# Loading and splitting the first block of a three-pass fp32 matmul kernel in smaller pieces

## The chip, the core and the metric

The kernel runs on one core of one Trainium2 chip. The metric is the device time of one execution in microseconds (us); of several runs the median is given. Beside the runs there is one profiled execution, whose trace is read here.

## What is computed

`x` is 64 samples of 64 channels by 1024 values, so 4096 rows of 1024. Each sample has a condition, which picks one of 16 matrices of 64 x 64. The reference, cut to what matters:

```python
y = einsum('bct,bcd->bdt', x, W[condition])            # mixes the 64 channels of a sample
logits = einsum('bsd,ed->bse', y, gate_w)              # 8 experts, the best 2 are kept
weights = softmax(top_k(logits, 2))                    # w_full: 8 numbers a row, 6 of them zero
result = einsum('bsd,od->bso', y, base_w) + base_b     # 1024 x 1024
low = einsum('bsd,erd->ebsr', y, lora_A)               # 8 experts x rank 16
lora = einsum('ebsr,eor,bse->bso', low, lora_B, w_full)
out = x + result + 2.0 * lora
```

## The kernel before

The mixing of channels is applied after the large product, since it acts on the other side of x. For each tile of 128 rows (two samples; there are 32 tiles) the kernel first forms z = x times one wide matrix of 1160 columns: 136 for the low-rank part and the gate, then the 1024 of `base_w`. It is cut into three column blocks of 384, 388 and 388 (`CN`; `W` is 388), and its 1024 rows into four quarters of 2 x 128 (`KQ` = 4). A weight block "b21" is quarter 2, column block 1, held as 128 partitions x 2 slices x 388 columns; a slice is one set of 128 rows, index `f` in the code. Likewise an x block is 128 partitions x 2 slices x 128.

Every fp32 operand is split into a high part, a copy rounded to the matmul's fp32r type, and a low part, the difference. Each product is then three matmuls into the same PSUM bank: high x times high weights, high x times low weights, low x times high weights. In the profile `xr` is x as loaded, `xh` and `xl` its parts; `w_b` is a weight block as loaded, `wh_b` and `wl_b` its parts. Line 232 is the copy that makes a high part (ScalarE, or VectorE for the first x blocks), line 229 the subtraction that makes a low part (VectorE), line 409 the three matmuls of z.

The first four tiles are multiplied plainly; the other 28 go in pairs through a 2 x 4 by 4 x 3 block product with fewer multiplications, made of sums of the blocks (line 290 for x, line 340 for weights). After z, line 441 mixes the channels and adds the low-rank part, line 492 is a transpose for it, and line 451 or 232 brings the result into `xtok`, from which it is stored.

The order on each engine is not written by hand. Steps are registered with `add(engine, cost, fn, reads, writes, ...)` in class `Program`; `reads` and `writes` are keys of buffers, from which it derives what depends on what. `run` then simulates the engines with the costs given and always issues, on the engine that comes free first, the step that is due earliest. Only after that are semaphores set. A key stands for the unit on which steps wait for each other: before the change an x block has one key, ("xr", u), and a weight block one key for each of its two slices, ("w", slot, f).

At the start, tiles 0 and 1 run together: for each quarter, column blocks 1 and 2, tile 0 before tile 1. The loads of the first weight block, b11, are issued from ScalarE's queue, one for each slice (line 319); all others and the loads of x (line 274) are issued from SP's queue, first the two x blocks of quarter 1, then the two slices of b12, then from b21 on alternately a weight block (line 324) and an x block. Behind the last weight blocks but one stands the load of `lb` (lora_B, into an `xtok` buffer, line 589), then eight loads of x for tiles 2 and 3, and then the last weight block, b23. Each transfer from these two queues takes one of eight completion semaphores in turn, so a load also waits until the transfer eight before it has landed. While the first data come, `NWARM` = 39 small matmuls on zeros (line 223) keep TensorE at work.

Of the kernel before, what the change touches and what calls it, by code (L numbers as in the profile page):

```python
# [20 lines left out]
P = 128  # L21
# [10 lines left out]
W = 388  # L32
N0 = NG + T - 2 * W
CN = (N0, W, W)
OUTS = ((NG, N0, 0), (0, W, N0 - NG), (0, W, N0 - NG + W))
KQ = 4
NPAIR = NT // 2
NPLAIN = 2
# [3 lines left out]
PE, ACT, DVE, POOL, SP = "PE", "ACT", "DVE", "POOL", "SP"  # L42
# [4 lines left out]
ISSUE = 0.45  # L47
# [30 lines left out]
class Program:  # L78
# [7 lines left out]
    def add(self, engine, cost, fn, reads=(), writes=(), due=None, first=False, size=0.0, early=None, port=False,  # L86
            after=0.0):

        n = len(self.steps)
        engine, cost = (e if isinstance(e, (list, tuple)) else [e] for e in (engine, cost))
        deps = set()
        for b in list(reads) + list(writes):
            if b in self.writer:
                deps.add(self.writer[b])
        for b in writes:
            deps.update(self.readers.get(b, ()))
        for b in reads:
            self.readers.setdefault(b, []).append(n)  # L100
        for b in writes:
            self.writer[b], self.readers[b] = n, []
        deps.discard(n)
        self.steps.append(dict(eng=dict(zip(engine, cost)), fn=fn, deps=deps, first=first, size=size, port=port,
                               lag=FLIGHT + QUEUE + size * DMA if size else 0.0, after=after,
                               due=self.horizon if due is None else due,
                               early=SP in engine and not reads if early is None else early))
# [59 lines left out]
def cond_ffn_kernel(ctx, tc, xT, x, idx, cw, wall, bias, lb, out):  # L167
# [21 lines left out]
    nc = tc.nc  # L189
# [4 lines left out]
    def many(n, shape, dt, name):  # L194
# [6 lines left out]
    xr = sb.tile([P, NXR, 2 * P], F32, name="xr")  # L201
    xh, xl = sb.tile([P, NXA, 2 * P], F32R, name="xh"), sb.tile([P, NXA, 2 * P], F32R, name="xl")
# [8 lines left out]
    bank = {nm: ps.tile([P, 512], F32, name=f"ps_{nm}")  # L211
            for nm in ("z0", "z1", "z2", "z3", "a0", "a1", "o0", "o1")}
# [13 lines left out]
    add = pr.add  # L226

    def sub(e, o, a, b):
        eng[e].tensor_tensor(o, a, b.bitcast(F32), ALU.subtract)  # L229

    def copy(e, o, a):
        (nc.scalar.copy if e == ACT else nc.vector.tensor_copy)(o, a)  # L232
# [7 lines left out]
    def tt_cost(n):  # L240
        return 0.08 + 0.00104 * n
# [22 lines left out]
    def some(t, us):  # L264

        a, b = us[0], us[-1]
        if len(us) == 1 or a < b:
            return t[:, a:b + 1:max(1, b - a)]
        return t[:, a:a + 1].broadcast_to([P, 2, t.shape[2]])


    def load_x(i, k, u):

        add(SP, ISSUE, lambda e: nc.sync.dma_start(  # L274
            xr[:, u].rearrange("p (k n) -> p k n", k=2), xT[i][:, 2 * k:2 * k + 2]), writes=[("xr", u)],
            size=8.0 * P * P)

    def split_x(us, hi=ACT):

        n = len(us)  # L280
        js = xas.two() if n == 2 else [xas.one()]
        add(hi, 0.1 + (0.115 if hi == ACT else 0.09) * 2 * n, lambda e: copy(e, some(xh, js), some(xr, us)),
            [("xr", u) for u in us], [("xh", j) for j in js])
        add(DVE, tt_cost(2 * P * n), lambda e: sub(e, some(xl, js), some(xr, us), some(xh, js)),
            [("xr", u) for u in us] + [("xh", j) for j in js], [("xl", j) for j in js], port=True)
        return js

    def sum_x(os, xs, ys, f):

        add(DVE, tt_cost(2 * P * len(os)), lambda e: nc.vector.tensor_tensor(some(xr, os), some(xr, xs), some(xr, ys), f),  # L290
            [("xr", u) for u in set(xs + ys) - set(os)], [("xr", u) for u in os], port=True)


    class Block:


        def __init__(self, name, dt=F32):
            self.name, self.dt, self.slot, self.t = name, dt, slots.one(), None
            self.keys = [("w", self.slot, f) for f in range(2)]

        def ap(self):
            if self.t is None:
# [3 lines left out]
    raw, hi, lo = {}, {}, {}  # L306
# [4 lines left out]
    def load_w(m):  # L311

        k, n = int(m[1]) - 1, int(m[2]) - 1
        b = raw[m] = Block(f"w_{m}")
        if k == 0 and n < 2:

            for f in range(2):
                q, dma = (SP, nc.sync.dma_start) if n else (ACT, nc.scalar.dma_start)
                add(q, ISSUE, lambda e, f=f, dma=dma: dma(b.ap()[:, f:f + 1], wall[k][n][:, f:f + 1]),
                    writes=b.keys[f:f + 1], size=4.0 * P * W, early=False)  # L320
            if not n:
                add(ACT, 1.5, lambda e: nc.scalar.activation(warm, warm, AF.Exp))
            return
        add(SP, ISSUE, lambda e: nc.sync.dma_start(b.ap(), wall[k][n]), writes=b.keys, size=8.0 * P * W, early=False)  # L324

    def split_w(m, p, step=2):

        b, h, l = raw[m], Block(f"wh_{m}_{p}", F32R), Block(f"wl_{m}_{p}", F32R)
        hi[p], lo[p] = h, l
        for j in range(0, 2, step):  # L330
            a = slice(j, j + step)
            add(ACT, 0.2 + 0.00083 * W * step, lambda e, a=a: copy(e, h.ap()[:, a], b.ap()[:, a]), b.keys[a], h.keys[a])
            add(DVE, tt_cost(W * step), lambda e, a=a: sub(e, l.ap()[:, a], b.ap()[:, a], h.ap()[:, a]),
                b.keys[a] + h.keys[a], l.keys[a], port=True)
# [25 lines left out]
    SINGLE = dict(b32="p1", b42="p2", b41="p12", b33="p11", b31="p20")  # L360
# [36 lines left out]
    due = {}  # L397

    def mm_cost(n):
        return max(COL * n + SET, LEAST)  # L400

    def zstep(key, b, j, p, f, start, stop, cols=W):


        z, n = bank[b][:, :cols], slice(f * P, (f + 1) * P)

        def do(e):
            for q, (l, w) in enumerate(((xh, h), (xh, g), (xl, h))):
                nc.tensor.matmul(z, l[:, j, n], w.ap()[:, f, :cols], start=(start and q == 0), stop=(stop and q == 2),  # L409
                                 skip_group_check=True)  # L410
        h, g = hi[p], lo[p]
        add(PE, 3 * mm_cost(cols), do, [("xh", j), ("xl", j), h.keys[f], g.keys[f]], [b, "order"], due=due[key])

    def split_z(n, src, key):

        q = take("zq", NZ)
        h, l = zh[q][:, :n], zl[q][:, :n]
        add(ACT, 0.2 + 0.00085 * n, lambda e: copy(e, h, src()), [key], [("zh", q)])
        add(DVE, 0.09 + 0.00104 * n, lambda e: sub(e, l, src(), h), [key, ("zh", q)], [("zl", q)],
            port=isinstance(key, tuple))  # L420
        return q

    def outs(c):

        lo, hi, o = OUTS[c]
        return slice(lo, hi), slice(o, o + hi - lo)
# [98 lines left out]

    PLAIN = [(i, c, k) for k in range(KQ) for c in range(2) for i in range(2)]
    PLAIN += [(i, 2, k) for i in range(2) for k in LASTK]
    for q in range(1, NPLAIN):
        PLAIN += [(i, c, k) for c in range(3) for i in (2 * q, 2 * q + 1) for k in range(KQ)]
    t = 4.9  # L530
# [23 lines left out]
    xa0 = {}  # L554
# [8 lines left out]
    def load_split_x(i, k, **how):  # L563
        u = xrs.one()
        load_x(i, k, u)
        xa0[i, k], = split_x([u], **how)
        xrs.give(u)

    for k in range(KQ):
        for i in range(2):  # L570
            load_split_x(i, k, hi=DVE if k == 0 else ACT)
            load_split_w(f"b{k + 1}{i + 1}", step=1 if k == 0 else 2)

    chan = sb.tile([P, 1], F32, name="chan")
# [20 lines left out]
    zb, left = {}, {}  # L595
# [3 lines left out]
    def plain(i, c, k):  # L599
        if (i, k) not in xa0:  # L600
            us = xrs.two()
            for d in range(2):
                load_x(i, k + d, us[d])
            xa0[i, k], xa0[i, k + 1] = split_x(us)
            xrs.give(*us)
        if (i, c) not in zb:
            zb[i, c] = f"z{take('z', 4)}"
            if c == 0 and i > 1:
                load_cond(i)
        ks, m = LASTK if c == 2 and i < 2 else range(KQ), f"b{k + 1}{c + 1}"  # L610
        for f in range(2):
            zstep(("plain", i, c, k, f), zb[i, c], xa0[i, k], SINGLE.get(m, m), f, k == ks[0] and f == 0,
                  k == ks[-1] and f == 1, CN[c])
        left[i, k] -= 1
        if not left[i, k]:
            xas.give(xa0[i, k])
        if k == ks[-1]:
            post(i, c, split_z(CN[c], lambda: bank[zb[i, c]][:, :CN[c]], zb[i, c]))
            if c == 2:
                late_sum(i)  # L620
                store(i, range(3))
# [74 lines left out]
    z = {nm: bank[b][:, :W] for nm, b in BANKS.items()}  # L696
# [153 lines left out]
```

## Time and profile before

| | us |
|---|---|
| median of 3 runs | 460.23 |
| lowest and highest | 459.87, 460.57 |
| profiled execution, its whole time | 460.46 |
| span of its trace | 458.7 |
| TensorE busy | 452.3 (99%) |
| VectorE busy | 383.4 (84%) |
| ScalarE busy | 227.5 (50%) |
| first matmul of z starts | 5.04 |
| first matmul of tile 1 starts | 7.11 |

Times within the trace count from the start of the span. In the profile PE is TensorE, PEld its weight loads, DVE is VectorE, ACT is ScalarE, POOL is GpSimd and SP the sync engine; PEq, ACTq and SPq are their sequencers, and a DMA on such a line is its issue. An instruction's line gives its start, its duration, the engine, the line of the kernel, the operation, and what it writes and reads; in brackets stands how long the engine was idle before it, and who ended that. Durations of matmuls overlap, so their pace is read from their starts.

### The profile page before, as it was taken

To read this page: it belongs to the slowest core of one execution; us is meant where nothing else is said; L and a number is where in the kernel's file an instruction comes from. 1 tells how busy PE (TensorE), PEld (TensorE's weight loads), DVE (VectorE), ACT (ScalarE), POOL (GpSimd) and SP (SyncE) were. 2 spreads that over 40 slices of the span, in tenths; PEclk is the share of its full clock that TensorE was granted. 3 is DMA by queue.
4 is the path that set the end of the run, shared out by engine and by line. 5 is a ranking of instruction groups with operands and counts; after the bars stand their busy time and mean duration, and the time that the engine had idled before them with its cause. 6 is when DMAs were issued, how large, how long until landed. Compare 5 with 4: busy or idle time off the path is not lost.

```text
span 458.7 us, 7562 instructions
## 1 busy us (share of the span) xinstructions
PE 452.3 (99%) x2615; PEld 449.0 (98%) x2615; DVE 383.4 (84%) x940; ACT 227.5 (50%) x520; POOL 88.8 (19%) x107
## 2 busy tenths in 40 slices
PE   8999999999999999999999999999999999999995
PEld 8999999999999999999999999999999999999995
DVE  5999997878989788796997979789797988888674
ACT  5864656543636345373543646355354544546231
POOL 3010215121303021120303003030120403103000
PEclk9999999999999999999999999999999999999999
DMA  8942739976778462764846566573655746456142
GB/s 284 336 126 42 160 98 205 214 215 198 176 211 202 172 161 88 215 128 167 188 137 189 119 185 150 172 181 110 196 120 177 182 128 195 114 176 148 48 137 91
DMA packets 36085, 75.00 MB, mean 164 GB/s; under 512 B 4416, under 2 KB 22096, under 8 KB 36048
## 3 DMA queue, kind: packets, MB, share of 16 engines
q0 software_dynamic: 10560, 36.72, 33.7%
q1 hardware_dynamic: 25200, 37.41, 26.0%
q10 hardware_dynamic: 288, 0.40, 0.3%
q8 instruction: 20, 0.33, 0.3%
q14 instruction: 17, 0.14, 0.1%
HBM read 57.74 MB, written 16.78 MB: 162 GB/s over the span
## 4 chain that ended last, share of the span: by engine, by line
PE 93%; DMA 5%; DVE 1%; SPq 1%; ACT 0%; issue 0%; ACTq 0%
PE ps_z L409 71%; PE ps_o L441 15%; PE ps_a L441 6%; DMA xtok<-in_lb 2%; DMA w_b<-in_w 2%; DMA xr<-in_xT 1%; PE ps_a L492 1%; SPq L324 0%; SPq L274 0%; DVE xtok L451 0%; DVE wl_b_b L229 0%; ACT wh_b_b L232 0%; DVE st L727 0%; ACTq L232 0%
## 5 line engine op out<-in xcount | busy, mean ns | idle before, releaser
L229 DVE TENSOR_TENSOR xl<-xr,xh 128x512 fp32r<-128x512 f32 (+1 forms) x138 | 92.3, 672 | 20.6 <-ACT xh L232 20.3
L409 PE MATMUL ps_z<-wh_t_p,xh 128*128 128x388 f32 (+1 forms) x308 | 105.3, 342 | 0.1
L409 PE MATMUL ps_z<-wl_t_p,xh 128*128 128x388 f32 (+1 forms) x308 | 104.3, 339 | 0.0
L409 PE MATMUL ps_z<-wh_t_p,xl 128*128 128x388 f32 (+1 forms) x308 | 104.3, 339 | 0.0
L232 ACT CAST xh<-xr 128x512 fp32r<-128x512 f32 (+1 forms) x136 | 82.5, 610 | 37.4 <-PE ps_z L409 32.8
L727 DVE TENSOR_TENSOR st<-ps_z,st 128x388 f32<-128x388 f32 x126 | 70.3, 559 | 21.0 <-PE ps_z L409 19.9
L290 DVE TENSOR_TENSOR xr<-xr 128x256 f32<-128x256 f32 (+1 forms) x139 | 69.7, 528 | 3.1 <-DMA xr<-in_xT 2.7
L409 PE MATMUL ps_z<-wh_b_p,xh 128*128 128x388 f32 (+1 forms) x180 | 61.4, 341 | 0.0
L409 PE MATMUL ps_z<-wh_b_p,xl 128*128 128x388 f32 (+1 forms) x180 | 60.8, 338 | 0.0
L409 PE MATMUL ps_z<-wl_b_p,xh 128*128 128x388 f32 (+1 forms) x180 | 60.8, 338 | 0.0
L409 PEld LDWEIGHTS ps_z<-wh_t_p,xh 128*128 128x128 f32 x308 | 57.8, 188 | 1.2 <-DVE st L727 0.7
L409 PEld LDWEIGHTS ps_z<-wl_t_p,xh 128*128 128x128 f32 x308 | 57.9, 188 | 0.0
L409 PEld LDWEIGHTS ps_z<-wh_t_p,xl 128*128 128x128 f32 x308 | 57.8, 188 | 0.0
L458 POOL DMA_DIRECT2D out<-xtok x30 | 16.8, 560 | 193.5 <-DVE xtok L451 92.2
L232 ACT CAST zh<-st 128x388 fp32r<-128x388 f32 (+1 forms) x70 | 36.2, 517 | 24.2 <-DVE st L727 17.0
L376 POOL DMA_DIRECT2D xtok<-in_bias x28 | 27.4, 980 | 97.3 <-DMA xtok<-in_x 90.0
L389 POOL DMA_INDIRECT bdr<-in_cw,rows x32 | 36.1, 1129 | 28.0 <-DVE zl L229 16.6
L710 ACT ACTIVATE ps_z<-ps_z 128x388 f32<-128x388 f32 x42 | 20.1, 478 | 41.1 <-PE ps_z L409 39.0
L451 DVE TENSOR_TENSOR xtok<-ps_o,xtok 128x388 f32<-128x388 f32 x56 | 31.0, 559 | 11.0 <-PE ps_o L441 10.6
L229 DVE TENSOR_TENSOR zl<-st,zh 128x388 fp32r<-128x388 f32 (+1 forms) x70 | 38.9, 556 | 1.5 <-ACT zh L232 1.2
L409 PEld LDWEIGHTS ps_z<-wh_b_p,xh 128*128 128x128 f32 x180 | 33.8, 188 | 0.2
L409 PEld LDWEIGHTS ps_z<-wl_b_p,xh 128*128 128x128 f32 x180 | 33.8, 188 | 0.0
(130 smaller groups left out, 871.1 us busy)
## 6 DMA issues: line engine op xcount, KB each, us to landing
xr<-in_xT SPq DMA_DIRECT2D x128, 128.0 KB, 3.1
xtok<-in_bias POOLq DMA_DIRECT2D x32, 512.0 KB, 7.2
out<-xtok POOLq DMA_DIRECT2D x30, 512.0 KB, 3.1
xtok<-in_x SPq DMA_DIRECT2D x28, 512.0 KB, 3.7
w_b<-in_w SPq DMA_DIRECT2D x10, 388.0 KB, 5.8
xtok<-in_x POOLq DMA_DIRECT2D x4, 512.0 KB, 6.2
out<-xtok SPq DMA_DIRECT2D x4, 194.0 KB, 2.5
bdr<-in_cw,rows POOLq DMA_INDIRECT x32, 5.3
```

What stands on the lines that cost most here:

```text
L229: eng[e].tensor_tensor(o, a, b.bitcast(F32), ALU.subtract)
L232: (nc.scalar.copy if e == ACT else nc.vector.tensor_copy)(o, a)
L290: add(DVE, tt_cost(2 * P * len(os)), lambda e: nc.vector.tensor_tensor(some(xr, os), some(xr, xs), some(xr, ys), f), [("xr", u) for u in s ...
L376: add(POOL, 1.1, lambda e: nc.gpsimd.dma_start(xtok[j], bias.broadcast_to([P, T]), accum_op=ALU.add), writes=keys, size=TWICE * 4.0 * T * P)
L389: add(POOL, 1.04, lambda e: nc.gpsimd.indirect_dma_start(out=bdr[j], out_offset=None, in_=cw, in_offset=bass.IndirectOffsetOnAxis(ap=rows[ ...
L409: nc.tensor.matmul(z, l[:, j, n], w.ap()[:, f, :cols], start=(start and q == 0), stop=(stop and q == 2), skip_group_check=True)
L441: nc.tensor.matmul(d, l, r, start=(start and m == 0), stop=(stop and m == len(mms) - 1), skip_group_check=True)
L451: add(DVE, 0.09 + 0.00104 * (s.stop - s.start), lambda e: nc.vector.tensor_tensor(xtok[j][:, o], bank[b][:, s], xtok[j][:, o], ALU.add), [ ...
L458: add(POOL, 1.0, lambda e: nc.gpsimd.dma_start(out[i * P:(i + 1) * P, o], xtok[j][:, o]), src, size=4.0 * P * (o.stop - o.start))
L492: add(PE, 0.107, lambda e: nc.tensor.matmul(tp, low[i % 2][:, :ER], ident, is_transpose=True, start=False, stop=False, skip_group_check=True),
L710: add(ACT, 0.2 + 0.00085 * W, lambda e: nc.scalar.mul(z[b], z[x], scale), [BANKS[x]], [BANKS[b]])
L727: add(DVE, 0.09 + 0.00104 * W, lambda e: nc.vector.tensor_tensor(unit(u), a(), b(), f), reads, [ukey(u)])
```

## The change

Slice 0 of the first weight block, b11, is treated as two halves of 194 columns; slice 1 stays whole. So b11 is loaded in three transfers instead of two, cast in three copies and subtracted in three subtractions. The first x block, tile 0 of quarter 1, is loaded as two slices of 128 in two transfers, cast in two copies on VectorE and subtracted in two. For tile 0 the three matmuls of b11's slice 0, 384 wide, become six of 194 (the four columns beyond 384 are padding). For that the keys are made finer: an x block has a key for each slice, a weight slice one for each half, and `add` accepts lists of keys. Everything else waits on all of the finer keys and does the same work as before. `NWARM` and the costs of all other steps are unchanged.

In the order that the planner makes of it, ScalarE issues the loads of b11 as first half of slice 0, slice 1, second half of slice 0, and casts and subtractions of b11 follow in the same sequence. TensorE's matmuls go first half, second half, slice 1. SP's queue has one transfer more at its head and ScalarE's one more at its own. One copy on ScalarE (`bdh`, the first tile's channel matrix) stands one weight block earlier than before. The rest of the program has the same order on every engine.

```diff
+HALVES = (slice(0, 194), slice(194, W))
...
+        reads, writes = ([k for q in ks for k in (q if isinstance(q, list) else [q])] for ks in (reads, writes))
...
     def load_x(i, k, u):
-        add(SP, ISSUE, lambda e: nc.sync.dma_start(
-            xr[:, u].rearrange("p (k n) -> p k n", k=2), xT[i][:, 2 * k:2 * k + 2]), writes=[("xr", u)],
-            size=8.0 * P * P)
+        for a, n in ((0, 1), (1, 1)) if (i, k) == (0, 0) else ((0, 2),):
+            add(SP, ISSUE, lambda e, a=a, n=n: nc.sync.dma_start(
+                xr[:, u, a * P:(a + n) * P].rearrange("p (k n) -> p k n", k=n),
+                xT[i][:, 2 * k + a:2 * k + a + n]), writes=xkeys("xr", [u])[a:a + n], size=4.0 * n * P * P)
...
+        if parts:
+            for f in range(2):
+                c, k, x, y, z = slice(f * P, (f + 1) * P), 0.1 + 0.09, ("xr", us[0], f), ("xh", js[0], f), ("xl", js[0], f)
+                add(hi, k, lambda e, c=c: copy(e, xh[:, js[0], c], xr[:, us[0], c]), [x], [y])
+                add(DVE, tt_cost(P), lambda e, c=c: sub(e, xl[:, js[0], c], xr[:, us[0], c], xh[:, js[0], c]),
+                    [x, y], [z], port=True)
+            return js
...
-                add(q, ISSUE, lambda e, f=f, dma=dma: dma(b.ap()[:, f:f + 1], wall[k][n][:, f:f + 1]),
-                    writes=b.keys[f:f + 1], size=4.0 * P * W, early=False)
+                for h in range(2) if (n, f) == (0, 0) else (None,):
+                    c = HALVES[h] if h is not None else slice(0, W)
+                    add(q, ISSUE, lambda e, f=f, c=c, dma=dma: dma(b.ap()[:, f, c], wall[k][n][:, f, c]),
+                        writes=[b.keys[f] if h is None else b.keys[f][h]], size=4.0 * P * (c.stop - c.start),
+                        early=False)
...
+        if m == "b11":
+            for f, c, k in ((0, HALVES[0], 0), (0, HALVES[1], 1), (1, slice(0, W), None)):
+                x, y, z = (t.keys[f] if k is None else t.keys[f][k] for t in (b, h, l))
+                n = c.stop - c.start
+                add(ACT, 0.2 + 0.00083 * n, lambda e, f=f, c=c: copy(e, h.ap()[:, f, c], b.ap()[:, f, c]), [x], [y])
+                add(DVE, tt_cost(n), lambda e, f=f, c=c: sub(e, l.ap()[:, f, c], b.ap()[:, f, c], h.ap()[:, f, c]),
+                    [x, y], [z], port=True)
+            return
...
-            zstep(("plain", i, c, k, f), zb[i, c], xa0[i, k], SINGLE.get(m, m), f, k == ks[0] and f == 0,
-                  k == ks[-1] and f == 1, CN[c])
+            for h in (0, 1) if (m, f) == ("b11", 0) and i == 0 else (None,):
+                zstep(("plain", i, c, k, f), zb[i, c], xa0[i, k], SINGLE.get(m, m), f, k == ks[0] and f == 0 and not h,
+                      k == ks[-1] and f == 1, CN[c], h)
```

## The prediction

> **What bounds the kernel now.** I read the page first, then the chain that ended last in order of time, then the instructions in order of time at both ends of that chain's first stretch. The page says that TensorE is busy throughout at a full granted clock, so a microsecond counts only if TensorE loses or wins it.
>
> ```profile
> span 458.7 us, 7562 instructions
> PE 452.3 (99%) x2615; PEld 449.0 (98%) x2615; DVE 383.4 (84%) x940; ACT 227.5 (50%) x520; POOL 88.8 (19%) x107
> PEclk9999999999999999999999999999999999999999
> DMA  8942739976778462764846566573655746456142
> ```
>
> The change touches only the first 7 us. The chain from 0 to 46 us shows what the first 27 us hang on: not TensorE but a string of transfers (columns: start, duration, what).
>
> ```profile
> 0.74 3.71 DMA w_b<-in_w
> ...
> 6.76 5.76 DMA xr<-in_xT
> ...
> 12.54 8.50 DMA xtok<-in_lb
> ...
> 21.51 3.63 DMA w_b<-in_w
> ...
> 25.24 0.85 ACT wh_b_b L232
> ...
> 26.12 0.98 DVE wl_b_b L229
> ...
> 27.14 2.74 PE ps_z L409 x14
> ```
>
> The transfer issued at 21.51 is the last weight block, b23. SP issues it only after eight x loads, the eighth of which waits for lb to land (21.04). Its cast and low part follow, and TensorE stands waiting:
>
> ```profile
> 26.50 0.34 PE L441 MATMUL ps_a<-zl,bdh 128*128 128x384 f32 x1
> 26.67 0.34 PE L409 MATMUL ps_z<-wh_b_b,xh 128*128 128x388 f32 x1
> 27.14 0.44 PE L409 MATMUL ps_z<-wl_b_b,xh 128*128 128x388 f32 x1
> 27.42 0.34 PE L409 MATMUL ps_z<-wh_b_b,xl 128*128 128x388 f32 x1
> ```
>
> Matmuls of this width start 0.175 us apart, so the one at 27.14 could have started at 26.845: it waits 0.295 us. Before it, from 6.94 on, they run without a gap. So TensorE reaches b23 with 0.295 us to spare: arriving earlier buys nothing, arriving later costs nothing up to that much. Only b23's own readiness moves the end one for one.
>
> The start itself, as it is now:
>
> ```profile
> 5.04 0.44 PE L409 MATMUL ps_z<-wh_b_b,xh 128*128 128x384 f32 x1
> 5.64 0.44 PE L409 MATMUL ps_z<-wl_b_b,xh 128*128 128x384 f32 x1 [0.15 <-DVE wl_b_b L229]
> 5.97 0.45 PE L409 MATMUL ps_z<-wh_b_b,xl 128*128 128x384 f32 x1
> 6.25 0.33 PE L409 MATMUL ps_z<-wh_b_b,xh 128*128 128x384 f32 x1
> 6.66 0.44 PE L409 MATMUL ps_z<-wl_b_b,xh 128*128 128x384 f32 x1
> 6.94 0.33 PE L409 MATMUL ps_z<-wh_b_b,xl 128*128 128x384 f32 x1
> 7.11 0.33 PE L409 MATMUL ps_z<-wh_b_b,xh 128*128 128x384 f32 x1
> ```
>
> Six matmuls take from 5.04 to 7.11, 2.07 us for 1.05 us of work. That 1.0 us is what the change goes for.
>
> **The change on TensorE.** It cannot begin much earlier: 39 warm-up matmuls stand ahead in its queue and their last weight load ends at 4.82, so the first real matmul moves from 5.04 to 4.87 at best. Three 384-wide matmuls become six of 194. The nearest narrower rows, 248 wide at 37.73, 37.84 and 37.96, are 0.113 us apart; I take that for 194 too (bounds 0.088, by width, and 0.175). 6 x 0.113 - 3 x 0.175 = +0.15 us of work.
>
> When do the pieces arrive? The first half of weight slice 0 (97 KB; I call it h0) and the first half of x (64 KB) are half of blocks that landed at 4.44 and 4.20. Some 0.6 us passes from last byte to landing (an estimate: the slices shown below sum to the first six transfers of now, 1,057 KB, at 5.65, and the sixth landed about 6.4). So the whole slice's bytes were there at about 3.85, when 360 KB had moved; half of that had moved at 3.3, and h0 lands 0.6 later, at 3.9; the same for x gives 3.7. Bounds are the landings of the whole blocks, and 3.0, where the rate first rises. In the instruction order of the changed kernel the ScalarE queue loads h0, then slice 1 whole, then the second half h1, and casts and subtractions follow that order. So h1 is the last of the same 388 KB, and lands where slice 1 lands now, 5.28; slice 1 comes about 4.85, between 4.44 and 5.28.
>
> ScalarE (rows: 0.29 for 128 columns, 0.40 for 256, 0.51 for 388; 0.35 for 194): h0 3.92 to 4.27, slice 1 4.87 to 5.38, h1 5.30 to 5.65. VectorE (subtraction rows: 0.29 for 128, 0.42 for 256, 0.56 for 388; 0.35 for 194; the cast of 128 is 0.2, below the 0.29 of 256): x's first cast and low part by 4.24, wl of h0 4.32 to 4.67, x's second half by 5.21, wl of slice 1 5.43 to 5.99, wl of h1 5.90 to 6.25. TensorE: three matmuls from 4.87, a stall to 5.70 for h1, a stall to 6.30 for its low part, then one of 194 and three of 384 with all operands there: 6.30 + 0.22 + 0.113 + 3 x 0.175 = 7.16. Tile 1's first matmul now starts at 7.11: TensorE is 0.05 us later, since the six small matmuls still wait for h1's low part, the last thing made. Bounds: no stall at all gives 4.87 + 6 x 0.113 + 3 x 0.175 = 6.07, 1.04 early; a low part as late as now's (6.61) gives 7.47, 0.36 late. At b23 TensorE arrives at 26.90 instead of 26.845, still 0.24 before the low part: cost nothing. Without that cover it would be 0.05 us.
>
> VectorE then gets to x of tile 1 at 6.2 instead of 5.83, low part by 6.95, used at 7.5; the low parts of b12 are done by 7.9, and first used at 8.33: covered. ScalarE issues a third transfer, 0.43 us, so its table load and warm-up end at 3.6 instead of 3.16, ahead of h0. On ScalarE one cast of 0.29 (bdh) also moves ahead of the cast of b41, into an idle of 0.71: nothing.
>
> **The change on the queues.** The one path that counts is the transfers. Each takes one of eight completion semaphores in turn, and waits for the one eight before it. Two more transfers at the head mean that SP's load of b21, issued at 2.59 without a wait, now waits for h0 (3.9), and the x load behind it goes from 3.07 to 4.35; the next ones issue about 0.4 us later. Who waits for these? The engines, if they run dry:
>
> ```profile
> GB/s 0 0 0 0 0 14 108 91 62 60 233 325 379 396 395 383 383 367 409 388 414 383 329 360 307 331 383 340 339 403 400 392 357 430 438 376 392 435 416 362
> ```
>
> These are slices of 0.3 us from 0 to 12. First bytes flow at about 1.75, 1.0 us after the first issue at 0.74. The first eight transfers now hold 1,057 KB, and the slices sum to that at 5.65. b21's first bytes come at 3.9 + 1.0 = 4.9, or 5.5 if h0 lands as late as the whole slice (4.44). Either way the stream has work: cost nothing, margin 0.15 to 0.75 us. From lb on both orders are alike: eight x loads, the eighth behind lb, then b23.
>
> The pieces add 256 packets, 16 an engine. Page part 3 gives 26.0% of 16 engines' span for 25,200 packets, 75.7 ns each; a full packet's price for each would be 1.2 us, the upper bound. Below, it is 0 if time goes by bytes. The windows 3:6 (small packets) and 9:12 (large) moved 366 and 400 GB/s, 9% apart; on the 0.5 MB that is split, 1.35 us of stream, that is 0.1 us. I take it, being nearest to these rows. It lands on lb, b23 and the end: +0.1.
>
> The Trainium skill's "DMA: Bandwidth & Descriptors", section Bandwidth, speaks against the change: transfers should be batched to 1 MiB, and those under 64 KB are ruled by descriptors; its table has 138 GB/s at 64 KB. By that, an estimate, the 131 KB of x would occupy 0.95 us of stream instead of 0.34, and the sum would be +0.6 us instead of +0.1. The slices above, with 128 KB transfers at 380 GB/s, rather show that queued transfers overlap; none of 64 KB is in this trace.
>
> **Sum.** The profiled execution took 460.46 us (span 458.7), 0.23 over the median of 460.23. 460.46 + 0.00 (TensorE) + 0.1 (stream) = 460.56; on the median's scale 460.3.
>
> **Rivals.** (1) Slower: the transfer stream loses time at the head, by the small packets or because b21 waits too long behind h0. It decides from h0 landing after 4.65, each further 0.1 us going straight to b23 (up to 0.4, at 5.05, a landing 0.6 beyond the whole slice's); packets alone can bring 1.2. The two together, +0.6 to +1.6, about 461.4. For: lb has no slack. Against: the rate stayed above 360 GB/s with mixed sizes. Chance 0.20. (2) TensorE arrives over 0.295 us late, because h1's low part waits longer in VectorE's queue: +0.1 to +1.0, 460.8. Chance 0.08. (3) Faster: b23 is ready earlier and TensorE too. The two would have to gain together: TensorE up to 1.04, and the stream, through a smoother start, up to as much; 459.4. Against: bytes and order ahead of lb are unchanged. Chance 0.08. (4) The forecast, in which the change doesn't do what it says because h1 comes last and b23's wait takes what remains: 460.1 to 460.6, chance 0.64.
>
> **Numbers.** A measurement of this kernel can tell about 0.2%, 0.92 us. Faster by more: rival 3 whole, 0.08. Slower by more: two thirds of rival 1, the part of its span above 0.92, and a quarter of rival 2: 0.15. Within: 0.77. The range 459.5 to 461.4 holds the forecast, rival 2 and half of rival 1, and leaves out 0.18.
>
> **What would show it.** Right: h1's matmuls wait until about 6.3, tile 1's first matmul starts within 0.3 us of 7.11, and the gap before b23's low part is still there, ending at 27.1 to 27.3. Wrong: tile 1 starts before 6.6 and the end moves with it, so b23 did not hold it; lb lands after 21.5, so the stream lost time; or the 194-wide matmuls are further apart than 0.175.

## The result and the profile after

| | before | after |
|---|---|---|
| median, us (11 runs each, same chip) | 460.23 | 461.24 |
| lowest and highest | 459.87, 460.69 | 460.52, 461.71 |
| profiled execution, whole time | 460.46 | 460.72 |
| span of its trace | 458.7 | 458.9 |
| first matmul of z | 5.04 | 5.16 |
| first matmul of tile 1 | 7.11 | 7.43 |
| last matmul | 453.57 | 454.07 |

The ratio after to before is 1.0019, with a 95% interval of 1.0010 to 1.0027. The changed kernel is slower, by just about the 0.2% that a measurement can tell. In a second comparison the ratio was 1.0021 (1.0011 to 1.0030). The profiled execution of after is 0.5 us quicker than its median, so its trace shows the loss only in part.

The page of after, the parts that answer to those shown of before:

```profile
span 458.9 us, 7575 instructions
PE 453.2 (99%) x2618; PEld 451.0 (98%) x2618; DVE 383.9 (84%) x943; ACT 228.2 (50%) x521; POOL 90.6 (20%) x107
```

TensorE is still the bound, and busy 0.9 us longer. Its chain of waits from 0 to 48 us has lost the transfers that it had before (columns: start, duration, what):

```profile
1.06 4.34 PE ps_o L226 x39
5.40 21.24 PE ps_z L437 x117
```

From the warm-up on it is TensorE alone (line 409 is now 437, 441 is 471). No piece of it is a load of b23: the gap that the prediction leaned on is gone, as the instructions around b23 show (columns: start, duration, engine, line, operation):

```profile
26.83 0.34 PE L471 MATMUL ps_a<-zl,bdh 128*128 128x384 f32 x1
27.00 0.34 PE L437 MATMUL ps_z<-wh_b_b,xh 128*128 128x388 f32 x1
27.18 0.34 PE L437 MATMUL ps_z<-wl_b_b,xh 128*128 128x388 f32 x1
27.36 0.33 PE L437 MATMUL ps_z<-wh_b_b,xl 128*128 128x388 f32 x1
```

All four are a normal step apart. TensorE comes 0.33 us later, and b23's low part was done at 26.97 (before: 27.09). The third matmul on b23 starts at 27.36, against 27.42 before. So up to here the profiled execution of after has lost nothing; yet its last matmul is 0.50 us later (first line before, second after, from the instructions in order of time):

```profile
453.57 0.34 PE L441 MATMUL ps_o<-zl,bdh 128*128 128x388 f32 x1
```

```profile
454.07 0.34 PE L471 MATMUL ps_o<-zl,bdh 128*128 128x388 f32 x1
```

From that matmul on b23 to the last one it took 426.15 us before and 426.71 after, in a stretch where both kernels issue the same instructions in the same order. The start of after:

```profile
5.16 0.51 PE L437 MATMUL ps_z<-wh_b_b,xh 128*128 128x194 f32 x1
5.46 0.41 PE L437 MATMUL ps_z<-wl_b_b,xh 128*128 128x194 f32 x1
...
5.89 0.52 PE L437 MATMUL ps_z<-wh_b_b,xh 128*128 128x194 f32 x1
6.27 0.53 PE L437 MATMUL ps_z<-wl_b_b,xh 128*128 128x194 f32 x1
6.60 0.42 PE L437 MATMUL ps_z<-wh_b_b,xl 128*128 128x194 f32 x1
...
7.43 0.34 PE L437 MATMUL ps_z<-wh_b_b,xh 128*128 128x384 f32 x1
```

The line left out starts at 5.68. The second half begins at 5.89, and its next matmul, at 6.27, has waited for the half's low part, as forecast. But steps of one half of slice 0 are 0.21 to 0.30 us here (5.46, 5.68, 5.89), not 0.11: in this execution TensorE ran at half pace until about 6.9, which hides the wait for the half's cast (done at 5.82). What the transfers did in the first 9 us (busy time of PE, PEld, DVE, ACT and POOL with counts, then granted clock, share of the DMA engines, GB/s), before and after:

```profile
0.00:9.00 9.00, 7.67 (x56) 6.78 (x57) 4.15 (x13) 4.70 (x8) 3.78 (x11) 1.00 0.76 253
```

```profile
0.00:9.00 9.00, 7.94 (x57) 7.81 (x58) 4.77 (x16) 4.96 (x9) 4.27 (x11) 1.00 0.77 238
```

The engines are as busy, but move 238 GB/s instead of 253: 15 x 9 = 135 KB less by 9 us, 0.34 us of stream at the 395 GB/s that after moves from 9 to 12.

### The profile page after: what moved, and what is told of

It is laid out like the page before. It is cut to its first block, busy times and chain, and to the rows that moved or that the text cites. A ratio compares the mean times of both kernels' runs of the same rounds, so it can differ in the third digit from the quotient of the medians.

```text
span 458.9 us, 7575 instructions
## 1 busy us (share of the span) xinstructions
PE 453.2 (99%) x2618; PEld 451.0 (98%) x2618; DVE 383.9 (84%) x943; ACT 228.2 (50%) x521; POOL 90.6 (20%) x107
## 4 chain that ended last, share of the span: by engine, by line
PE 98%; DVE 1%; issue 0%
PE ps_z L437 76%; PE ps_o L471 15%; PE ps_a L471 6%; PE ps_o L226 1%; PE ps_a L522 1%; DVE st L758 0%; DVE xtok L481 0%; DVE zl L232 0%; DVE ltl L219 0%; DVE low L222 0%; DVE warm L324 0%
## 5 line engine op out<-in xcount | busy, mean ns | idle before, releaser
L232 DVE TENSOR_TENSOR xl<-xr,xh 128x512 fp32r<-128x512 f32 (+2 forms) x139 | 92.3, 666 | 20.8 <-ACT xh L235 20.5
L416 POOL DMA_INDIRECT bdr<-in_cw,rows x32 | 38.0, 1187 | 27.0 <-DVE zl L232 17.7
L437 PEld LDWEIGHTS ps_z<-wh_b_p,xl 128*128 128x128 f32 x180 | 33.9, 188 | 0.0
```

Source lines behind the costliest of these rows:

```text
L416: add(POOL, 1.04, lambda e: nc.gpsimd.indirect_dma_start(out=bdr[j], out_offset=None, in_=cw, in_offset=bass.IndirectOffsetOnAxis(ap=rows[ ...
L437: nc.tensor.matmul(z, l[:, j, n], w.ap()[:, f, cols], start=(start and q == 0), stop=(stop and q == 2), skip_group_check=True)
```

## The experiments

Two differences are in these traces that the change did not mean to make: a slower transfer stream at the start, and a slower pace of equal matmuls later on. For the second there is a candidate in the code. A weight buffer gets its place in SBUF at its first use (`Block.ap`), and the planner's changed order at the start changes the order of first uses. The orders of before and after differ in seven pairs of neighbours: fourteen buffers change places in pairs, 2 x 388 x 4 = 3,104 bytes further on or back, and with them the some thirty blocks that are held in them in turn. The first four runs separate the two.

**Addresses and start apart.** `c_before` and `c_after` are the two kernels as they are. `b_layA` is the kernel before with the buffer places of after, and `a_layB` the changed kernel with the places of before. The edit only fixes the order in which the first buffers get their places; no engine's instructions change. Here it is for `a_layB`; in `b_layA` the names stand in the order of after:

```diff
+            firsts.setdefault(name, self)
...
+    for nm in ("w_b11 w_b12 w_b21 w_b22 wh_b11_b11 w_b31 wl_b11_b11 w_b32 wh_b12_b12 w_b41 wl_b12_b12 w_b42 wh_b21_b21 w_b43 wl_b21_b21 w_b33 wh_b22_b22").split():
+        firsts[nm].ap()
     pr.run()
```

Expected of `c_before`: 

> The kernel before, once more, for a second trace. Measure: the stretch from the third matmul on b23 (27.42 in the first trace, 27.36 in the changed kernel's) to the last matmul (453.57, 454.07): 426.15 us before, 426.71 after. If the 0.56 us between them is a property of each kernel (theory: buffer addresses), the stretch is 426.1 to 426.3 again. If it is scatter between executions, it may as well come out at 426.7.

Expected of `b_layA`: 

> The kernel before, same instructions in the same order, with the weight buffers placed at the addresses that they have in the changed kernel (17 first uses in that order; some thirty names move by 3104 bytes). Theory of addresses: the stretch rises to about 426.7 and the time by about 0.5 us, ratio 1.0010 to 1.0013. Theory that the whole loss lies in the first 7 us (narrow matmuls at the low clock): stretch 426.15, ratio 1.0000 within 0.0005.

Expected of `a_layB`: 

> The changed kernel, same instructions in the same order, with the weight buffers at the addresses of the kernel before. Theory of addresses: the stretch falls to 426.15 and what stays against the kernel before is the start alone, 0 to 0.4 us, ratio 1.0000 to 1.0008. Theory of the start alone: nothing changes against the changed kernel, ratio 1.0019.

Expected of `c_after`: 

> The changed kernel once more, for a second trace. Ratio about 1.0019 as measured. Stretch 426.6 to 426.8 if it belongs to the kernel. In the first trace TensorE ran at the low rate until 6.9 us, in the trace of before until 4.4; if that moment varies from run to run it will lie elsewhere here, and with it the first matmul of tile 1 (7.43 in the first trace).

| run | median, us | ratio to before (95%) | last matmul | third b23 matmul to last |
|---|---|---|---|---|
| kernel before, same chip, 32 runs | 460.28 | | | |
| c_before | 460.29 | 1.0000 (0.9991 to 1.0009) | 453.48 | 426.27 |
| b_layA | 460.73 | 1.0009 (1.0000 to 1.0018) | 454.08 | 426.70 |
| a_layB | 460.73 | 1.0015 (1.0006 to 1.0024) | 453.67 | 426.23 |
| c_after | 461.23 | 1.0021 (1.0011 to 1.0030) | 454.33 | 426.67 |

The last column is the time from the start of the third matmul on b23 (27.21, 27.38, 27.44 and 27.66) to that of the last. It goes with the places alone: 426.15 to 426.27 us with those of before, in three profiles, and 426.67 to 426.71 with those of after, in three, whichever the kernel. In this stretch all of them issue the same matmuls in the same order, and so do six of the later runs, all with the places of before (`e1`, `e4`, `g1`, `g2`, `f3` and `f5` below): they took 426.16 to 426.35. The last matmul of `b_layA`, the kernel before with nothing moved but buffers:

```profile
454.08 0.34 PE L444 MATMUL ps_o<-zl,bdh 128*128 128x388 f32 x1
```

The means of three and three differ by 0.48 us over some 2,450 matmuls, 0.2 ns on each. It isn't one stall: in medians over the profiles of each kind no step between two matmuls grew by over 0.02 us, and the difference builds up little by little, to 0.28 us by 200 us and 0.52 by 400. Which buffers do it is open; no run moved them one by one. The times alone would not show it: `a_layB` was expected at a ratio of 1.0000 to 1.0008 if the places count, and its 1.0015 lies above that, with an interval that overlaps that of `c_after`. The stretches carry this reading.

The other half of the loss, 460.73 less 460.28, stays in `a_layB`, so it belongs to the start. The trace of `c_after`, whose execution took 461.12 us, shows one way in which it is paid. Its tile 1 begins early, at 7.03, and then five steps between matmuls are longer than usual, two of them (before 11.07 and 12.44) right behind a wait:

```profile
10.46 0.44 PE L437 MATMUL ps_z<-wl_b_b,xh 128*128 128x384 f32 x1
10.79 0.45 PE L437 MATMUL ps_z<-wh_b_b,xl 128*128 128x384 f32 x1
...
11.78 0.34 PE L437 MATMUL ps_z<-wl_b_b,xh 128*128 128x384 f32 x1
12.16 0.44 PE L437 MATMUL ps_z<-wh_b_b,xl 128*128 128x384 f32 x1
```

Beyond the step of 0.175, this sums to 0.66 us between 10.2 and 12.5; in `c_before` no step there is noticeably longer. VectorE's instructions in the same stretch show for what:

```profile
9.43 0.97 DVE L232 TENSOR_TENSOR wl_b_b<-w_b,wh_b_b 128x776 fp32r<-128x776 f32 x1 [1.70 <-ACT wh_b_b L235]
10.32 0.42 DVE L232 TENSOR_TENSOR xl<-xr,xh 128x256 fp32r<-128x256 f32 x1
10.81 0.97 DVE L232 TENSOR_TENSOR wl_b_b<-w_b,wh_b_b 128x776 fp32r<-128x776 f32 x1
11.69 0.42 DVE L232 TENSOR_TENSOR xl<-xr,xh 128x256 fp32r<-128x256 f32 x1
```

The matmul at 10.46 waits for b21's low part, the one at 10.79 for that of tile 0's x behind it, the one at 12.16 for that of tile 1's x, which stands behind b22's. And VectorE itself was idle for 1.70 us before b21, for ScalarE's cast. ScalarE's casts of whole weight blocks start as soon as a block has landed and the cast before is done. Those of b21, b22 and b31 start at 7.39, 9.21 and 10.54 in `c_before`, and at 8.56, 9.94 and 11.49 in `c_after`: 1.2, 0.7 and 0.95 us later (first `c_before`, then `c_after`):

```profile
7.39 0.84 ACT L232 CAST wh_b_b<-w_b 128x776 fp32r<-128x776 f32 x1 [0.57 <-DMA w_b<-in_w]
...
9.21 0.84 ACT L232 CAST wh_b_b<-w_b 128x776 fp32r<-128x776 f32 x1 [0.67 <-DMA w_b<-in_w]
...
10.54 0.84 ACT L232 CAST wh_b_p<-w_b 128x776 fp32r<-128x776 f32 x1 [0.19 <-DMA w_b<-in_w]
```

```profile
8.56 0.84 ACT L235 CAST wh_b_b<-w_b 128x776 fp32r<-128x776 f32 x1 [1.73 <-DMA w_b<-in_w]
...
9.94 0.84 ACT L235 CAST wh_b_b<-w_b 128x776 fp32r<-128x776 f32 x1 [0.23 <-DMA w_b<-in_w]
...
11.49 0.84 ACT L235 CAST wh_b_p<-w_b 128x776 fp32r<-128x776 f32 x1 [0.41 <-DMA w_b<-in_w]
```

**Which part of the start.** All further kernels have the buffer places of before. `e1_loads_whole` is the changed kernel with whole loads; casts, low parts and matmuls stay split:

```diff
-        for a, n in ((0, 1), (1, 1)) if (i, k) == (0, 0) else ((0, 2),):
+        for a, n in ((0, 2),):
...
-                for h in range(2) if (n, f) == (0, 0) else (None,):
+                for h in (None,):
```

> The changed kernel, with the weight buffers at the addresses they have in the kernel before, and with the first block of x and of the weights loaded whole again (one transfer of 128 KB, two of 194 KB, as before); casts, low parts and the first matmuls stay split. The same kernel with split loads took 460.73 us, the kernel before 460.28. Theory A (the transfers): what is left of the loss beside the addresses comes from the three added transfers and their smaller pieces at the head of the queues, which delay the stream. Then this one returns to 460.3 (460.0 to 460.5), the windows between 6 and 8.5 us move as many bytes as in the kernel before, and lb and b23 are issued and land as in it. Theory B (the second half of slice 0 comes last): whole loads bring that half with the first, so tile 1's first matmul starts near 7.0 instead of 7.4, and the time is 460.3 too. Theory C (the split of casts and matmuls itself costs): it stays at 460.7, with tile 1 after 7.3.

`e4_h1_first` keeps the split loads, but brings the second half of slice 0 ahead of slice 1:

```diff
-                        early=False)
+                        early=False, due=h - 9.0 if h is not None else None)
```

> The changed kernel with the addresses of the kernel before, and with the two halves of weight slice 0 loaded, cast and subtracted ahead of slice 1 (in the changed kernel the second half comes after slice 1). Number and sizes of transfers stay those of the change. Theory A (the transfers): nothing is won at b23, the time stays at 460.6 to 460.8, the stream between 6 and 8.5 us is as slow as in the changed kernel. Theory B (the second half comes last and holds TensorE): the stalls before the second half's matmuls go, tile 1's first matmul starts at 6.7 to 7.1, TensorE reaches b23 before its low part again and waits there, and the time is 460.2 to 460.4.

`g1_x_whole` makes only the first of e1's two edits (x whole, weights split), `g2_w_whole` only the second.

Expected of `g1_x_whole`: 

> The changed kernel with the addresses of before; the first x block is loaded whole, weight slice 0 in two halves, the second after slice 1, as in the change. The question is which of the split loads slows the stream: by 9 us the kernel before and the one with whole loads had moved 2.27 to 2.31 MB in five profiles, those with both split 2.10 to 2.18 MB in five. If the 512-byte packets of the x halves cost it: 2.27 to 2.31 MB by 9 us here, and 460.1 to 460.3. If the weight halves (776-byte packets, a third issue on ScalarE, the second half last) cost it: 2.10 to 2.20 MB and 460.4 to 460.7.

Expected of `g2_w_whole`: 

> The other half of the question: the first x block in two loads, weight slice 0 whole, addresses of before. If the x halves cost the stream: 2.10 to 2.20 MB by 9 us, and 460.4 to 460.7. If the weight halves do: 2.27 to 2.31 MB, and 460.1 to 460.3. If it is the count of transfers in the first eight, both runs lie between.

The kernel before had a median of 460.05 beside e1 and e4, and of 460.30 beside g1 and g2. Columns four to seven are of the profiled execution of each run; f1 to f5 follow below. All but the last row have the buffer places of before.

| kernel | median, us | ratio to before (95%) | profiled execution, us | GB/s, 0 to 9 us | cast of b22, of b31 | tile 1 |
|---|---|---|---|---|---|---|
| first block loaded whole: | | | | | | |
| before (first profile) | 460.23 | | 460.46 | 253 | 9.01, 10.56 | 7.11 |
| c_before | 460.29 | 1.0000 (0.9991 to 1.0009) | 460.29 | 256 | 9.21, 10.54 | 6.95 |
| e1_loads_whole | 460.16 | 1.0001 (0.9992 to 1.0010) | 460.23 | 252 | 9.37, 10.75 | 7.33 |
| f3_b23_moved | 460.14 | 0.9997 (0.9989 to 1.0006) | 460.06 | 253 | 9.20, 10.55 | 6.84 |
| f5_whole_b23 | 460.20 | 0.9998 (0.9989 to 1.0006) | 460.11 | 250 | 9.26, 10.69 | 7.16 |
| in pieces: | | | | | | |
| g1_x_whole | 460.69 | 1.0010 (1.0002 to 1.0019) | 460.33 | 244 | 9.40, 10.70 | 7.33 |
| g2_w_whole | 460.80 | 1.0012 (1.0003 to 1.0021) | 460.24 | 241 | 9.36, 10.89 | 6.71 |
| e4_h1_first | 460.46 | 1.0009 (1.0000 to 1.0018) | 460.31 | 241 | 9.59, 10.92 | 7.38 |
| a_layB | 460.73 | 1.0015 (1.0006 to 1.0024) | 460.34 | 242 | 9.71, 11.08 | 7.39 |
| after (first profile) | 461.24 | 1.0019 (1.0010 to 1.0027) | 460.72 | 238 | 9.37, 10.99 | 7.43 |

Theory A holds in its main point: with whole loads and everything else split, the loss is gone. Its signs in the trace came only in part. By 9 us `e1_loads_whole` has moved as much as the kernel before; but it gains that before 6 us, and from 6 to 8.5 it moves 306 GB/s, like `a_layB` (304) and below the kernel before (356 and 340). Two more profiles with whole loads (`b_layA` 257, `f1_b23_early` 253 GB/s) and two with pieces (`c_after` 234, `f2_both` 242) fall on the same two sides: seven from 250 to 257, seven from 234 to 244. The order of the pieces matters less: `e4_h1_first` has no stall before the second half, and its ratio is still 1.0009, with less moved by 9 us, though from 6 to 8.5 us its stream is not slow (341 GB/s). Its 460.46 lies between the numbers of theory A and theory B, 0.4 above the kernel before beside it; tile 1 (6.7 to 7.1 by theory B) came at 7.38, since slice 1 now landed last, so this run alone doesn't part the two. And theory C, that the split of casts and matmuls costs by itself, falls with e1.

Either load in pieces brings most of the loss: `g1_x_whole` and `g2_w_whole` each lie at +0.4 to +0.5 us, as both together do, so the costs do not add up. By 9 us they move 2.20 and 2.17 MB (GB/s times 9), both less than the 2.25 to 2.31 of whole loads. Neither the x halves nor the weight halves alone are the culprit; the times of these two and of `a_layB` can't be told apart. What the two have in common is one transfer more at the head and a smaller piece; no run parts number from size.

That tile 1 starts early isn't worth anything with pieces: in `g2_w_whole` it starts at 6.71, the earliest of those in pieces, and TensorE loses it again, waiting for 0.38 us between 11.3 and 11.9. This also speaks against theory B. Two runs with whole loads that began early show the same in small (`f3_b23_moved` 0.1 us at 11.7, `f1_b23_early` 0.2). Where tile 1 starts at 7.3 or later, as in after, `g1_x_whole` and `e4_h1_first`, TensorE doesn't wait there at all: then the late start itself has used up the time.

How the slower stream becomes a longer time is therefore seen in one execution only, that of `c_after`. The profiled executions of `a_layB`, `e4_h1_first`, `g1_x_whole` and `g2_w_whole` all have the slower stream, yet at 460.24 to 460.34 they are quicker than their own medians and within the range of the kernel before. In `g2_w_whole` the wait at 11 us is covered at b23, which holds TensorE for 0.34 us. The loss in the medians comes from executions that were not traced: those of `a_layB` go from 460.14 to 461.85, those of the kernel before beside it from 459.83 to 460.81. Nor do the casts of b22 part the two groups (9.37 in `e1_loads_whole`, 9.36 in `g2_w_whole`). That the pieces cost time is shown by the medians; by what path, in most executions, is not.

**What b23 holds.** The prediction took it that only b23's readiness keeps the matmuls near 27 us. `f1_b23_early` is the kernel before with the x loads of tiles 2 and 3 behind b23's load:

```diff
-                load_x(i, k + d, us[d])
+                load_x(i, k + d, us[d], after=18.0 if i < 4 else 0.0)
```

> The kernel before, with the eight x loads of tiles 2 and 3 issued after b23's load instead of ahead of it; nothing at the start is changed. It tests what the prediction rested on: that only b23's readiness holds the matmuls near 27 us, for 0.295 us. Theory of the prediction: b23 is cast and its low part made 2 us or more earlier, the gap before the matmul at 27.14 goes, and the time falls by up to 0.3 us, to 460.0, unless the x loads that now come later are waited for in its place. Rival: the gap is not what sets the end (TensorE makes it up or loses it again at the next tiles): 460.3.

It took 461.38 us, ratio 1.0035 (1.0021 to 1.0049): neither theory. At b23 the first one held: the third matmul starts at 26.92, with no gap, against 27.21 in `c_before`, and 0.25 us is still won at 34 us. Then come stalls that `c_before` doesn't have:

```profile
81.21 0.45 PE L412 MATMUL ps_z<-wh_t_p,xh 128*128 128x388 f32 x1 [0.22 <-ACT ps_z L713]
...
84.00 0.44 PE L412 MATMUL ps_z<-wh_t_p,xh 128*128 128x384 f32 x1 [0.39 <-DVE st L730]
```

With other times for the loads the planner had put all later tiles in another order, and its chain runs here through a late x load. The edit was not the one thing it was meant to be. `f2_both` has the same edit on top of `e4_h1_first`:

> The changed kernel with the addresses of the kernel before, the two halves of slice 0 ahead of slice 1, and b23's load issued ahead of the eight x loads of tiles 2 and 3. Without b23's wait, whatever TensorE wins at the start should reach the end. If splitting the first block helps TensorE at all: tile 1's first matmul at 6.4 to 6.8, no gap at b23, and 459.5 to 459.9. If splitting only costs: no better than the kernel before with b23 early, 460.0 or above.

It took 462.18 us, ratio 1.0040 (1.0027 to 1.0054). That is within "460.0 or above", but it says little on splitting, since it has the same late stalls as `f1_b23_early`, and in the profiled execution slice 1 is cast only at 6.61, against 5.75 in `e4_h1_first`, with the same instructions up to there. Tile 1 started at 8.24. How late a given piece lands varies that much from one execution to the next.

`f3_b23_moved` moves b23's load in the finished order instead, so that no other engine's order changes. `f5_whole_b23` does the same to e1:

```diff
-            steps[i]["fn"](e)
+            plan.append((i, e))
...
+        for i, e in rest[:q] + [(self.b23, SP)] + xs + rest[q:]:
+            steps[i]["fn"](e)
```

Expected of `f3_b23_moved`: 

> The kernel before with one thing moved: SP's load of b23 goes ahead of the eight x loads of tiles 2 and 3, in the written-out order, so that no instruction of another engine changes its place (in the earlier try the planner also reordered all later tiles, and a stall of 1.2 us between 73 and 86 us came with it). Theory: b23's readiness alone held the matmuls near 27 us; the gap of 0.2 to 0.3 us before its low part goes, nothing else moves, and the time is 459.8 to 460.0, with the last matmul 0.2 to 0.3 us earlier than in the kernel before. Rival: the x loads that come 4 us later hold tiles 2 and 3 instead, between 28 and 50 us: 460.3 or slower.

Expected of `f5_whole_b23`: 

> The changed kernel with the addresses of before, whole loads of the first block (casts, low parts and first matmuls stay split), and b23's load moved as in the run beside it. Without b23's wait a gain or loss of TensorE at the start reaches the end. If splitting the casts and matmuls helps where the loads cost nothing: 0.1 to 0.4 us below the kernel before with b23 moved, 459.5 to 459.8, with tile 1's first matmul at 6.6 to 6.9. If not (TensorE still at its low rate then, or operands no earlier): as that kernel or up to 0.3 slower.

The matmuls at b23 in `f3_b23_moved`:

```profile
26.52 0.34 PE L421 MATMUL ps_z<-wh_b_b,xh 128*128 128x388 f32 x1
26.70 0.40 PE L421 MATMUL ps_z<-wl_b_b,xh 128*128 128x388 f32 x1
26.94 0.34 PE L421 MATMUL ps_z<-wh_b_b,xl 128*128 128x388 f32 x1
```

The gap is down to 0.065 us, the third matmul is 0.27 earlier than in `c_before`, and 0.19 of it is left at the last one (453.29). The runs can't tell it: 460.14 beside 460.30, ratio 0.9997 (0.9989 to 1.0006). So b23 did hold the matmuls, for about the time the prediction read from the trace, and that is worth at most 0.2 us here. `f5_whole_b23`, with b23 out of the way and the first block's casts and matmuls split, took 460.20, inside the interval of f3's. With tile 1 at 7.16 the splitting gained nothing that could reach the end. No kernel of these is faster than the kernel before by more than the measurement tells.

## Why the prediction was right or wrong

**The number.** Forecast were 460.3 us and "same" (within 0.2%); measured was 461.24, a ratio of 1.0019. The range held it, 0.16 below its upper end, and the class was right by a hair. The centre was 0.9 us too low, and the likeliest case was not what happened.

**"h1 comes last": right, a term mis-sized.** The second half did land last and held its matmuls. It landed later than the 5.28 of the estimate: its cast starts at 5.47 in after and 5.72 in `a_layB`. The narrow matmuls were not 0.113 us apart in after, since TensorE was at half pace, and tile 1 started at 7.43 instead of 7.16, just outside the 0.3 us around 7.11 that was to speak for the forecast. Steps of over 0.175 us were even named as a sign against it; what they show here is the pace of that one execution. In `a_layB`, at full pace, the 194-wide ones are 0.11 apart, as taken from the 248-wide rows, and the wait for the half alone makes tile 1 late:

```profile
5.10 0.27 PE L440 MATMUL ps_z<-wl_b_b,xh 128*128 128x194 f32 x1
5.21 0.27 PE L440 MATMUL ps_z<-wh_b_b,xl 128*128 128x194 f32 x1
6.12 0.35 PE L440 MATMUL ps_z<-wh_b_b,xh 128*128 128x194 f32 x1 [0.64 <-ACT wh_b_b L235]
```

**"At b23 TensorE ... cost nothing": held in the first profile, for another reason, and too broad.** There TensorE was 0.32 us late at tile 1 and on time at b23. But the sign given for it, a gap that ends at 27.1 to 27.3, is missing: b23's load was issued at 21.12 instead of 21.51, its low part came earlier, and TensorE's lateness just filled the gap. In `c_after` TensorE is at b23's third matmul at 27.66, 0.24 to 0.45 after the kernel before, and the cover is used up. The prediction asked for one cover at 27 us and overlooked that an early TensorE can lose its lead at 10 to 12 us, ahead of it (`c_after` and `g2_w_whole`).

**"Who waits for these? The engines, if they run dry": the step that failed.** The text saw that b21's issue moves from 2.59 to 3.9 (it came at 3.82) and the next ones by about 0.4. It then asked only whether the transfer engines run dry, and took it that they don't. From 6 to 9 us their busy share was 1.03 before, 0.98 in after and 0.92 in `c_after`, there with 0.82 from 7 to 8 us: hardly dry, but not quite full either. In `c_after` the ones that wait are the casts of b21, b22 and b31, and behind them TensorE at 10 to 12 us. It priced the stream at +0.1 us. The stream was 0.34 us behind at 9 us, and the start costs about 0.45 us in the medians (`a_layB`; nothing in `e1_loads_whole`). The nearest rows, windows of mixed packets against windows of large ones, gave too small a price for the pieces. They could not give one: in the kernel before the window from 6 to 9 us, behind the small packets, moved 359 GB/s, less than the 366 of the window with them, and the slices shown fall to 307, so that the rate did not stay "above 360". The Trainium skill, "DMA: Bandwidth & Descriptors", section Bandwidth, spoke against small transfers, and the estimate from its figures was +0.6; the runs lie between, nearer to the rule.

**Rival 1** (the stream loses time at the head) named half of the cause. That its number, 461.4, is near to what was measured is luck: the stream's part, about 0.45 us, lies below the +0.6 to +1.6 it stated, and the buffers' places made up the rest. Its mechanism was not what the runs show either: it was to decide by h0 landing after 4.65 and to be paid at lb and b23. h0's cast starts at 3.83, and lb's issue does come 0.7 us later (13.25 for 12.54), yet b23's comes 0.4 us earlier. In `c_after` the price is paid at b21, b22 and the x blocks behind them. **Rivals 2 and 3** did not come: VectorE's queue is not what held the second half, and nothing got faster. (The "quarter of rival 2" above 0.92 us is a tenth of its span; the chances shift by 0.01.)

**What no case held: the buffers' places.** Half of the loss, 0.45 to 0.5 us, comes from matmuls that the change doesn't touch. The diff says nothing of it; only the change in the order of first uses does, which the order of the casts, read for the prediction, could have told.

**Still open.** Why the stream stays slow after the pieces have landed: in after it moves 262 GB/s from 7 to 8 us (before: 328), when the last piece has been there since about 5.4. Late issues alone are not it, since `g1_x_whole` issues b21 as before (2.60 for 2.59) and b22 earlier (4.22 for 4.46), and casts b22 later (9.40 for 9.01). Also open are how the loss reaches the end in the executions that make up the medians, and which of the moved buffers slows the matmuls.

## What to carry to other kernels

When a change delays a queue, don't ask only whether the engines of that queue run dry, but follow each later transfer to its first reader: in `c_after` the transfer engines were busy for 92% of the time from 6 to 9 us, and the third weight block was 1.2 us late all the same. A gap that hides one delay hides only what comes to it; look for every earlier point at which the same resource (here the arrival of weights) sets the pace. One trace can be of a quick execution: compare its time with the median before reading a loss, or none, from it. And where a pool gives out buffers in the order of first use, a change of order also moves buffers: pin the places before explaining a difference of 0.1%.

## What the runs showed of the hardware

The pace of matmuls with equal shapes and order depends on where the weight buffers lie in SBUF, slightly: 426.15 to 426.35 us for the stretch with one set of places, in nine profiles, and 426.67 to 426.71 with another, in three, 0.1%.

TensorE's first real matmuls may run at half pace although 39 warm-up matmuls stand ahead: 194 columns took 0.21 us a step in after until about 6.9 us and 0.11 in `a_layB` from 5.1 on, and the windows of the profile show a granted clock of 1.00 in both. The Trainium skill, "TensorE: Matmul & The Clock Gate", Part 1, says that the moment of the change to full rate varies from run to run, since the window that decides it runs free of the kernel's start; these two traces agree, and so does `c_after`, which has the instructions of after but a step of 0.11 us at 6.4. The moments lie some 1.8 us apart, more than the half microsecond either way that the section gives.

Splitting one of two early transfers, of 128 or 194 KB, lowered the stream's rate over the first 9 us from 250 to 257 GB/s to 241 to 244; with both split it was 234 to 242.
